# A two-bank Gelu in the perceptron of a window-attention layer on one Trainium2 core

## The chip, the cores and the metric

The kernel runs on one core of one Trainium2 chip. The metric is the device time of one launch in microseconds, as the median of several runs; lower is better. Of the core's engines four do the work here: PE (TensorE, matrix products; its weight loads are listed apart as PEld), ACT (ScalarE, functions from a table), DVE (VectorE) and SP (SyncE, which issues nearly all DMAs).

## The reference, cut to what matters

Four layers follow each other on x of shape (4, 16, 512, 512) in f32. The change is in layer 0 alone; layers 1 to 3 (convolutions with batch norm, a residual block, and a perceptron over channels) are left as they are.

```python
# layer 0
x = x + depthwise_conv3x3(x, pos_w) + pos_b
for each 8x8 window (64 tokens of 16 channels), 2 heads of 8:
    q, k, v = split(affine1(window) @ qkv_w.T + qkv_b)
    out = softmax(q * 8**-0.5 @ k.T) @ v
x = x + out @ proj_w.T + proj_b
h1 = gelu(affine2(x) @ fc1_w.T + fc1_b)     # 16 -> 64 channels
x = x + h1 @ fc2_w.T + fc2_b                # 64 -> 16 channels
```

## The kernel before, in words

`window_attention` does layer 0. The 128 partitions are four groups of 32 (index u, the batch), each of two window rows of 16 channels. A turn n of the main loop takes 64 columns and 8 rows in four places of the image (index vv): for each u and vv, 8 windows of 64 tokens in each of two window rows, so 512 columns of tokens per u and vv. There are 64 turns. The order on PE, DVE, ACT and SP is the order in which the code issues (`manual_schedule`)[...]. Waits are put in by the framework, which knows who wrote and who read each tile.

PSUM has eight banks of 128 x 512 f32. Before, banks 0 to 3 are two tiles of two banks each (`pairs`), and banks 4 to 7 are four tiles of their own (`singles`); `bank(i)` gives bank i of either.

A turn n runs so:

1. `values` (L348, transposes on PE, copied by DVE at L353) and `scores` (L361, into the pairs; Exp on ACT, L369) start the attention of n; between the first and the second `scores` stands `output` of turn n-1 (L428 on PE into banks 5, 7, 4, 6; L433 on DVE adds the residual into `xo`).
2. Seven rounds of `scores`, `attend` (L380, L385 into banks 4 and 5, or 6 and 7), `values` and `divide` (Ln and Exp on ACT at L394 and L395, a product on DVE at L396).
3. `queries` of turn n+1 in two halves (L330; DVE L340 and ACT L338 copy them out to `g`), with the last `attend` and `divide` between.
4. `project` (L404): 32 products into banks 4 to 7, one bank for each u; DVE (L409) adds bank 4+u to `y[:, u]`, four instructions one after the other.
5. The perceptron's first layer for turn n, mixed with the depthwise convolution of turn n+2. 52 slots follow each other. A slot is either one `depthwise` turn (L297: four products of 32x32 by 512 columns, one tap, one u, into bank u of the first two pairs) or one `hidden` turn (L417: four such products with fc1 for one u and vv, into one of banks 4 to 7, then Gelu on ACT at L422 into a `hid` tile). The profile counts each of these f32 products as two records. Slot i works on row group i % 4 of PE. The 16 `hidden` turns stand at slots 4, 6, 9, 11, 14, 16, ..., 36, 39, 41; the other 36 slots are the nine taps of the four u. In the last two turns there is no depthwise work left.
6. The table for Ln and Exp is asked for on ACT (L549), and `position(n + 2)` takes the depthwise result out of the pairs into y: DVE for u = 0 and 2 (L312), ACT for u = 1 and 3 (L308). The next turn's `scores` write into the same pairs.

The table for Gelu is loaded where the first Gelu of a turn needs it; the framework puts the load there (it appears under L422).

Of the kernel before, what the change touches and what calls it, by code (L numbers as in the profile page):

```python
# [12 lines left out]
F32 = mybir.dt.float32  # L13
BF16 = mybir.dt.bfloat16
AF = mybir.ActivationFunctionType
# [10 lines left out]
P = 128  # L26
# [128 lines left out]
def window_attention(ctx: ExitStack, tc, xw, x1, hots, m, v, peak):  # L155
# [14 lines left out]
    nc = tc.nc  # L170
    U = V = 4
    BW = 64
    NJ = BW // WS
    N = NJ * T
# [3 lines left out]
    STEPS = SR // WS * NQ * 2  # L178

    wts = ctx.enter_context(tc.tile_pool(name="w0w", bufs=1))  # L180
    ps = ctx.enter_context(tc.tile_pool(name="w0p", bufs=1, space=PSUM))

    pairs = [ps.tile([P, 2, 512], F32, name=f"pair{i}") for i in range(2)]
    singles = [ps.tile([P, 512], F32, name=f"bank{i}") for i in range(4)]

    def bank(i):
        return pairs[i // 2][:, i % 2, :] if i < 4 else singles[i - 4]

    def quad(i):
        return slice(32 * i, 32 * i + 32)  # L190
# [3 lines left out]
    def load(k):  # L194
        t = xin.tile([P, V, WS + 2, XW + 2], F32, tag="x", name=f"x{k}")
        nc.sync.dma_start(t, xw[k])
        return t
# [6 lines left out]
    def prod(lhsT, rhs, name, n=P):  # L204

        b = bank(7)[:, 0:n]
        nc.tensor.matmul(b, lhsT, rhs, start=True, stop=True)
        t = scratch.tile([P, n], F32, name=name)
        nc.vector.tensor_copy(t, b)
        return t  # L210

    def times(a, s, name):
        t = scratch.tile(list(a.shape), F32, name=name)
        nc.vector.tensor_scalar(t, a, s, None, ALU.mult)
        return t

    def plus(a, b, name, pool=None):
        t = (pool or scratch).tile(list(a.shape), F32, name=name)
        nc.vector.tensor_tensor(t, a, b, ALU.add)
        return t  # L220

    def kept(a, name):
        t = wts.tile(list(a.shape), F32, name=name)
        nc.vector.tensor_copy(t, a)
        return t
# [8 lines left out]
    with tc.tile_pool(name="w0s", bufs=1) as scratch:  # L234
# [11 lines left out]
        for h in range(NH):  # L246
# [11 lines left out]
        fc1 = kept(prod(m("color2"), times(m("fc1"), v("alpha2"), "fc1_a"), "fc1_0"), "fc1_e")  # L258
        f1b = plus(
            prod(m("fc1")[0:32], v("beta2")[0:32], "f1_b", 1), v("fc1_b"), "f1b"  # L260
        )

        pb = plus(pb, v("fc2_b"), "pb2", wts)
        f1b = plus(f1b, prod(fc1[0:32], times(v("fc2_b"), -1.0, "f2n")[0:32], "f2_b", 1), "f1b2", wts)
# [8 lines left out]
    px = ctx.enter_context(tc.tile_pool(name="w0x", bufs=2))  # L273
# [12 lines left out]
    def by_window(ap):  # L286
        return ap.rearrange("p (j a x) -> p a j x", a=WS, x=WS)
# [39 lines left out]
    def queries(y, h):  # L327
        for u in range(U):
            for vv in range(V):
                nc.tensor.matmul(  # L330
                    bank(vv)[quad(u)], wg[h][quad(vv)], y[quad(vv), u, :],
                    start=True, stop=True,
                )
        for vv in range(V):
            out = g[:, vv, :, h, :]
            src = bank(vv).rearrange("p (j t) -> p j t", t=T)
            if vv % 2:
                nc.scalar.activation(out, src, AF.Identity, bias=gb[:, h : h + 1])  # L338
            else:
                nc.vector.tensor_scalar(out, src, gb[:, h : h + 1], None, ALU.add)  # L340


    def values(k, n):

        vv, jl = k // 2, 4 * (k % 2)
        b = bank(4 + 2 * (k % 2))
        for jj in range(4):
            nc.tensor.transpose(  # L348
                b[:, P * jj : P * jj + P],
                y2[:, vv, jl + jj].rearrange("p w t -> p (w t)"), m("ident"),  # L350
            )
        t = px.tile([P, 4, P], F32, tag="yt", name=f"yt{n}_{k}", bufs=3)
        nc.vector.tensor_copy(t.rearrange("p j c -> p (j c)"), b)  # L353
        return t

    def scores(k, n):

        vv, jl = k // 2, 4 * (k % 2)
        for jj in range(4):
            for u in range(U):  # L360
                nc.tensor.matmul(  # L361
                    bank(u)[:, P * jj : P * jj + P],
                    y2[quad(u), vv, jl + jj].rearrange("p w t -> p (w t)"),
                    g[quad(u), vv, jl + jj].rearrange("p h t -> p (h t)"),
                    start=True, stop=True,
                )
        e = px.tile([P, U, 4, P], F32, tag="e", name=f"e{n}_{k}", bufs=3)
        for i in range(2):
            nc.scalar.activation(  # L369
                e[:, 2 * i : 2 * i + 2].rearrange("p u j t -> p u (j t)"),  # L370
                pairs[i], AF.Exp,
            )
        return e
# [36 lines left out]
                y[:, u], bank(4 + u), pb, y[:, u], ALU.add, ALU.add  # L410
            )

    def hidden(y, q, vv, n):

        u, b = q // 4, bank(4 + q % 4)
        for k in range(4):
            nc.tensor.matmul(  # L417
                b[quad(k)], fc1[quad(vv), quad(k)], y[quad(vv), u, :],
                start=True, stop=True,
            )  # L420
        hd = px.tile([P, N], F32, tag="hid", name=f"hid{n}_{u}_{vv}", bufs=16)
        nc.scalar.activation(hd, b, AF.Gelu, bias=f1b)  # L422
        return vv, hd

    def output(y, xo, hids, us, banks, n):

        for k, (vv, hd) in enumerate(hids):
            nc.tensor.matmul(  # L428
                bank(banks[k // 4])[quad(vv)], m("fc2"), hd, start=True, stop=True
            )  # L430
        at = BW * (n % 2)
        for u, i in zip(us, banks):
            nc.vector.tensor_tensor(  # L433
                xo[:, u, :, at : at + BW].rearrange("p a (j x) -> p a j x", x=WS),
                by_window(bank(i)), by_window(y[:, u]), ALU.add,
            )
            if n % 2:
                store(xo, n // 2, u)
# [6 lines left out]
    def store(xo, k, u):  # L445
        i, cb = divmod(k, NQ)
        largest.append(
            lambda: nc.vector.tensor_reduce(
                peak[:, U * k + u : U * k + u + 1], xo[:, u], AX.XY, ALU.max,
                apply_absolute_value=True,  # L450
            )
        )
        for vv in range(V):
            for w in range(2):
                r = SR * (2 * vv + w) + WS * i
                _store_block(
                    nc, x1, xo[32 * vv + C * w : 32 * vv + C * w + C, u], u, r,
                    slice(XW * cb, XW * cb + XW), queues if k == STEPS // 2 - 1 else None,
                )
# [35 lines left out]
    last, xo = None, None  # L495
    nc.scalar.preload_act_table_set("natural_log_exp_and_others")
    for n in range(STEPS):
        yts = {k: values(k, n) for k in range(2)}
        es = {0: scores(0, n)}
        if last:  # L500

            output(*last)
        for k in range(1, 8):
            es[k] = scores(k, n)
            attend(es[k - 1], yts[k - 1], k - 1)
            if k > 1:
                yts[k] = values(k, n)
            divide(k - 1, n)
            if k == 3:
                nc.vector.tensor_reduce(  # L510
                    most[:, n : n + 1], ys[n], AX.XY, ALU.max, apply_absolute_value=True
                )
            elif largest:
                largest.pop(0)()
            if k % 2 and n + 1 < STEPS:
                turn_keys(ys[n + 1], k // 2)
        if n + 1 < STEPS:
            queries(ys[n + 1], 0)
        attend(es[7], yts[7], 7)
        divide(7, n)  # L520
        if n + 1 < STEPS:
            queries(ys[n + 1], 1)
        y = ys.pop(n)
        project(y)

        ahead = n + 2 < STEPS
        if ahead and n % 2 == 0 and n // 2 + 2 < STEPS // 2:
            xts[n // 2 + 2] = load(n // 2 + 2)
        if n % 2 == 0:
            xo = px.tile([P, U, WS, XW], F32, tag="xo", name=f"xo{n}", bufs=1)  # L530
        if n + 1 == STEPS:
            flag = bounded()

        at = [4 + 10 * u + d for u in range(U) for d in (0, 2, 5, 7)]
        hids, taken = [], [0] * U
        for i in range(13 * 4):
            if i in at:
                q = len(hids)  # L540
                hids.append(hidden(y, q, i % 4, n))
                if n + 1 == STEPS and q in (5, 9, 13):
                    u = q // 4 - 1
                    output(y, xo, hids[q - 5 : q - 1], (u,), (u,), n)
            elif ahead:
                depthwise(n + 2, taken[i % 4], i % 4)
                taken[i % 4] += 1
        if n + 1 < STEPS:
            nc.scalar.preload_act_table_set("natural_log_exp_and_others")  # L549
        if ahead:  # L550
            ys[n + 2] = position(n + 2)
        last = (y, xo, hids, range(U), (5, 7, 4, 6), n)
# [822 lines left out]
```

## Time and profile before

| what | value |
|---|---|
| three runs | 6373.32, 6380.44, 6388.24 us; median 6380.44 us |
| span of the profiled execution, first to last instruction | 6371.6 us |
| its own time beyond the span | not shown by the page |
| mean granted TensorE clock | 0.983 |
| 0 to 3400 us (layer 0) | PE busy 3333 us, ACT 2627 us, DVE 1574 us, clock 1.00 |
| 3560 to 6371 us (later layers) | PE busy 2695 us, ACT 1329 us, DVE 1541 us, clock 0.98 |

The profile is of one execution of the program. "Busy" means that at least one instruction of the engine was in flight: products on PE are pipelined and overlap, so a PE busy all the time may still be waiting between products. The time of a turn can be read off a timeline, whose start column counts from the first instruction of the span. One turn of the loop, the one near 1000 us, serves as the example below:

| stretch of that turn, us | what runs on PE | PE busy | DVE busy | ACT busy |
|---|---|---|---|---|
| 1002.30 to 1003.66 | end of project, first depthwise slots | 1.36 | 0.81 | 0.60 |
| 1003.66 to 1014.50 | fc1 and depthwise slots | 10.84 | 1.92 | 10.70 |
| 1014.50 to 1016.87 | depthwise slots | 2.37 | 0.27 | 1.95 |
| 1016.87 to 1019.95 | transposes, first scores | 2.68 | 2.34 | 1.49 |
| 1019.95 to 1024.50 | output, second scores | 4.55 | 2.77 | 1.79 |
| 1024.50 to 1052.00 | the attention's rounds, queries, project | 27.50 | 16.95 | 23.55 |

### The profile page before, as it was taken

To read this page: it belongs to the slowest core of one execution; us is meant where nothing else is said; L and a number is where in the kernel's file an instruction comes from. 1 tells how busy PE (TensorE), PEld (TensorE's weight loads), DVE (VectorE), ACT (ScalarE), POOL (GpSimd) and SP (SyncE) were. 2 spreads that over 40 slices of the span, in tenths; PEclk is the share of its full clock that TensorE was granted. 3 is DMA by queue.
4 is the path that set the end of the run, shared out by engine and by line. 5 is a ranking of instruction groups with operands and counts; after the bars stand their busy time and mean duration, and the time that the engine had idled before them with its cause. 6 is when DMAs were issued, how large, how long until landed. Compare 5 with 4: busy or idle time off the path is not lost. (4 is left out here: it accounts for less than half of the span.)

```text
span 6371.6 us, 316872 instructions
## 1 busy us (share of the span) xinstructions
PE 6125.4 (96%) x146976; PEld 3619.7 (57%) x146976; DVE 3189.7 (50%) x4713; ACT 4035.4 (63%) x5602; POOL 151.0 (2%) x127
## 2 busy tenths in 40 slices
PE   8999999999999999999997569999999999999999
PEld 4666666666666666666663445455555555555554
DVE  3444444444444444444444665555555555555555
ACT  4777777777777777777776544444444444444444
POOL 0000000000000000000002510000000000000000
PEclk9999999999999999999998789999999999999999
DMA  3233323333333333333323732222222222222221
GB/s 81 59 76 61 76 60 75 61 75 61 75 61 75 62 74 62 73 63 73 62 57 108 295 129 76 82 82 87 85 83 84 82 83 83 84 83 83 83 72 51
DMA packets 567526, 515.29 MB, mean 81 GB/s; under 512 B 349009, under 2 KB 478353, under 8 KB 545713
## 3 DMA queue, kind: packets, MB, share of 16 engines
q1 hardware_dynamic: 564688, 493.47, 29.7%
q8 instruction: 1154, 18.91, 1.3%
q0 software_dynamic: 1216, 1.05, 0.1%
q14 instruction: 180, 1.47, 0.1%
q10 hardware_dynamic: 288, 0.39, 0.0%
HBM read 225.87 MB, written 134.48 MB: 57 GB/s over the span
## 5 line engine op out<-in xcount | busy, mean ns | idle before, releaser
L1166 ACT ACTIVATE hid<-tb,vec 128x512 f32<-128x512 f32 x1280 | 830.6, 689 | 1061.0 <-PE tb L1160 1058.1
L1160 PE MATMUL tb<-y,mat 32*32 32x512 f32 x16384 | 1498.8, 596 | 2.0 <-issue 1.5
L369 ACT ACTIVATE e<-pair 128x1024 f32<-128x1024 f32 x1024 | 992.5, 1021 | 396.3 <-PE pair L361 396.3
L1168 DVE TENSOR_SCALAR hid<-tb,vec 128x512 f32<-128x512 f32 x768 | 574.7, 749 | 739.1 <-PE tb L1160 732.9
L297 PE MATMUL pair<-x,taps 32*32 32x512 f32 x18432 | 927.9, 605 | 2.4 <-ACT y L308 1.2
L417 PE MATMUL bank<-y,fc_e 32*32 32x512 f32 x8192 | 680.3, 598 | 1.3 <-DVE y L409 0.9
L361 PE MATMUL pair<-g,y 32*128 32x128 f32 x16384 | 654.0, 285 | 27.1 <-ACT y L308 24.5
L361 PEld LDWEIGHTS pair<-g,y 32*128 32x128 f32 x16384 | 544.1, 187 | 216.1 <-issue 110.8
L297 PEld LDWEIGHTS pair<-x,taps 32*32 32x32 f32 x18432 | 601.8, 103 | 98.5 <-issue 18.8
L422 ACT ACTIVATE hid<-bank,f1b 128x512 f32<-128x512 f32 x1024 | 644.2, 686 | 13.0 <-PE bank L417 5.5
L930 PE MATMUL tb<-z,cw 32*32 32x512 f32 x12864 | 635.2, 600 | 5.4 <-issue 4.1
L353 DVE COPY yt<-bank 128x512 f32<-128x512 f32 x512 | 347.8, 689 | 552.2 <-PE bank L348 533.1
L1160 PEld LDWEIGHTS tb<-y,mat 32*32 32x32 f32 x16384 | 466.5, 103 | 264.1 <-issue 149.8
L930 PE MATMUL tb<-h,cw 32*32 32x512 f32 x12672 | 567.9, 597 | 4.4 <-issue 2.8
L930 PE MATMUL tb<-x,cw 32*32 32x512 f32 x12480 | 562.4, 597 | 1.4 <-ACT z L1099 1.4
L380 PE MATMUL bank<-e,yt 128*32 128x128 f32 x16384 | 557.4, 276 | 3.6 <-issue 2.1
L930 PE MATMUL tb<-q,cq 32*32 32x512 bf16 x12672 | 420.2, 454 | 140.8 <-issue 63.2
L396 DVE TENSOR_TENSOR o<-bank,r 128x512 f32<-128x512 f32 x512 | 354.3, 692 | 372.4 <-ACT r L395 356.2
L385 PE MATMUL bank<-e,hot 128*32 128x512 f32 x4096 | 535.9, 593 | 0.0
L380 PEld LDWEIGHTS bank<-e,yt 128*32 128x32 f32 x16384 | 418.2, 109 | 112.4 <-DVE yt L353 52.8
L1176 PE MATMUL tb<-hid,mat 128*32 128x512 f32 x4096 | 452.7, 594 | 0.0
L312 DVE TENSOR_SCALAR y<-pair,vec 128x512 f32<-128x512 f32 x128 | 90.3, 747 | 707.1 <-PE pair L297 707.1
(163 smaller groups left out, 6689.3 us busy)
## 6 DMA issues: line engine op xcount, KB each, us to landing
x<-in_xw_dram SPq DMA_DIRECT2D x32, 2600.0 KB, 11.0
y<-y SPq DMA_DIRECT2D x2048, 32.0 KB, 2.2
tx<-x SPq DMA_DIRECT2D x64, 1024.0 KB, 5.6
xi<-x SPq DMA_DIRECT2D x1024, 64.0 KB, 2.4
out_dram<-xi SPq DMA_DIRECT2D x64, 1024.0 KB, 4.6
x<-xo SPq DMA_DIRECT2D x1974, 32.0 KB, 1.7
y<-x SPq DMA_DIRECT2D x24, 1024.0 KB, 4.9
xi<-x SPq DMA_DIRECT2D x24, 1024.0 KB, 4.9
```

The costliest lines, as they stand in the source:

```text
L297: nc.tensor.matmul(bank(u)[quad(vv)], taps[quad(u), tap, :], xts[n // 2][quad(u), vv, dy : dy + WS, at : at + BW], start=tap == 0, stop=ta ...
L361: nc.tensor.matmul(bank(u)[:, P * jj : P * jj + P], y2[quad(u), vv, jl + jj].rearrange("p w t -> p (w t)"), g[quad(u), vv, jl + jj].rearra ...
L369: nc.scalar.activation(e[:, 2 * i : 2 * i + 2].rearrange("p u j t -> p u (j t)"), pairs[i], AF.Exp,)
L380: nc.tensor.matmul(b[quad(u), P * jj : P * jj + P], yt[:, jj, quad(u)], e[:, u, jj, :], start=True, stop=True,)
L385: nc.tensor.matmul(d[quad(u)], own, e[:, u].rearrange("p j t -> p (j t)"), start=True, stop=True,)
L417: nc.tensor.matmul(b[quad(k)], fc1[quad(vv), quad(k)], y[quad(vv), u, :], start=True, stop=True,)
L422: nc.scalar.activation(hd, b, AF.Gelu, bias=f1b)
L930: nc.tensor.matmul(p[i][_quad(j)], weights[_quad(i), side, dx, :], src[side][_quad(i), j, dx : dx + W], start=side == 0 and dx == 0, stop= ...
L1160: nc.tensor.matmul(p[_quad(c)], w1[_quad(b), 1 - par, 32 * c : 32 * c + 32], inner(ys(mm + par))[_quad(b), s, :], start=True, stop=True,)
L1166: nc.scalar.activation(hd, p, AF.Relu, bias=v("l3_b1"))
L1168: nc.vector.tensor_scalar(hd, p, v("l3_b1"), 0.0, ALU.add, ALU.max)
L1176: nc.tensor.matmul(p[_quad(b), :], w2[:, par], hd, start=par == 0, stop=par == 1)
```

## The change

All eight banks of layer 0 become four pairs: banks 4 and 5 are one tile, and so are 6 and 7. `hidden` takes two vv at once: eight products into the two banks of a pair, then one Gelu over 128 x 1024 into one `hid` tile of twice the size (half as many buffers, so the same memory). A turn has eight such double turns, at slots 4, 10, 16, ..., 46, each taking the place of two slots; the four slots between two of them stay depthwise. The order of row groups, i % 4, stays as it was. The table for Gelu is asked for explicitly behind the second half of `queries`, ahead of `project`. In the last turn, the calls of `output` follow the new count.

```diff
-    pairs = [ps.tile([P, 2, 512], F32, name=f"pair{i}") for i in range(2)]
-    singles = [ps.tile([P, 512], F32, name=f"bank{i}") for i in range(4)]
+    pairs = [ps.tile([P, 2, 512], F32, name=f"pair{i}") for i in range(4)]
 
     def bank(i):
-        return pairs[i // 2][:, i % 2, :] if i < 4 else singles[i - 4]
+        return pairs[i // 2][:, i % 2, :]
...
-    def hidden(y, q, vv, n):
-
-        u, b = q // 4, bank(4 + q % 4)
-        for k in range(4):
-            nc.tensor.matmul(
-                b[quad(k)], fc1[quad(vv), quad(k)], y[quad(vv), u, :],
-                start=True, stop=True,
-            )
-        hd = px.tile([P, N], F32, tag="hid", name=f"hid{n}_{u}_{vv}", bufs=16)
-        nc.scalar.activation(hd, b, AF.Gelu, bias=f1b)
-        return vv, hd
+    def hidden(y, q, vvs, n):
+
+        u, pair = q // 4, pairs[2 + q // 2 % 2]
+        for j, vv in enumerate(vvs):
+            for k in range(4):
+                nc.tensor.matmul(
+                    pair[quad(k), j], fc1[quad(vv), quad(k)], y[quad(vv), u, :],
+                    start=True, stop=True,
+                )
+        hd = px.tile([P, 2, N], F32, tag="hid", name=f"hid{n}_{q}", bufs=8)
+        nc.scalar.activation(hd, pair, AF.Gelu, bias=f1b)
+        return [(vv, hd[:, j]) for j, vv in enumerate(vvs)]
...
             queries(ys[n + 1], 1)
+        nc.scalar.preload_act_table_set("gelu_and_others")
         y = ys.pop(n)
         project(y)
...
-        at = [4 + 10 * u + d for u in range(U) for d in (0, 2, 5, 7)]
+        at = range(4, 52, 6)
         hids, taken = [], [0] * U
         for i in range(13 * 4):
             if i in at:
                 q = len(hids)
-                hids.append(hidden(y, q, i % 4, n))
-                if n + 1 == STEPS and q in (5, 9, 13):
+                hids += hidden(y, q, (i % 4, i % 4 + 1), n)
+                if n + 1 == STEPS and q in (4, 8, 12):
                     u = q // 4 - 1
-                    output(y, xo, hids[q - 5 : q - 1], (u,), (u,), n)
-            elif ahead:
+                    output(y, xo, hids[q - 4 : q], (u,), (u,), n)
+            elif i - 1 not in at and ahead:
                 depthwise(n + 2, taken[i % 4], i % 4)
                 taken[i % 4] += 1
```

## The prediction

> **What bounds the kernel now.** I read the page first, then the timelines of PE, ACT and DVE over one turn of layer 0's loop (the 64 turns repeat to a few ns; their period is 52.7 or 53.0 us), then who waited for line 308.
>
> ```profile
> span 6371.6 us, 316872 instructions
> PE 6125.4 (96%) x146976; PEld 3619.7 (57%) x146976; DVE 3189.7 (50%) x4713; ACT 4035.4 (63%) x5602; POOL 151.0 (2%) x127
> L422 ACT ACTIVATE hid<-bank,f1b 128x512 f32<-128x512 f32 x1024 | 644.2, 686 | 13.0 <-PE bank L417 5.5
> ```
>
> PE is 96% busy and ACT 63%: shares alone say that a shorter Gelu (L422) saves nothing unless PE waits for it. So the order inside a turn decides. ACT from the end of the queries to the next attention (columns: start, time covered, line and operation, idle before and what ended it):
>
> ```profile
> 1001.55 1.35 ACT L338 ACTIVATE g<-pair,gb 128x512 f32<-128x512 f32 x2 [1.42 <-DVE g L340]
> 1003.68 1.28 ACT L422 ACT_TABLE_LOAD   x1 [0.78 <-DVE y L409]
> 1004.98 10.19 ACT L422 ACTIVATE hid<-bank,f1b 128x512 f32<-128x512 f32 x16
> 1015.18 1.28 ACT L549 ACT_TABLE_LOAD   x1
> 1017.39 1.34 ACT L308 ACTIVATE y<-pair,vec 128x512 f32<-128x512 f32 x2 [0.92 <-DVE y L312]
> ```
>
> ACT looks saturated by Gelus (16 in 10.19 us, one per 0.634), yet it finishes, loads Exp's table and then sits idle 0.92 us before y (L308). PE and DVE over the same stretch:
>
> ```profile
> 1003.66 0.63 PE L417 MATMUL bank<-y,fc_e 32*32 32x512 f32 x4
> 1004.11 0.61 PE L417 MATMUL bank<-y,fc_e 32*32 32x512 f32 x4
> 1013.26 0.66 PE L417 MATMUL bank<-y,fc_e 32*32 32x512 f32 x6
> 1013.78 3.09 PE L297 MATMUL pair<-x,taps 32*32 32x512 f32 x73
> 1018.13 0.49 PE L361 MATMUL pair<-g,y 32*128 32x128 f32 x4 [0.23 <-ACT y L308]
> 1002.85 2.73 DVE L409 SCALAR_TENSOR_TENSOR y<-bank,pb,y 128x512 f32<-128x512 f32 x4 [0.68 <-PE bank L404]
> 1016.60 1.41 DVE L312 TENSOR_SCALAR y<-pair,vec 128x512 f32<-128x512 f32 x2 [11.02 <-PE pair L297]
> ```
>
> The reader is to see the chain: depthwise ends (last record starts 1016.28), DVE y (1016.60 to 1017.35), ACT y (1017.39), scores (L361, 1018.13). The loop numbers 52 slots per turn, each 8 matmul records (four products, each two records); slots 0 to 3 are depthwise, slot 4 is the first fc1 turn. Is PE paced by ACT in there? Two rows say no. The fc1 turn of slot 41 begins at 1013.26 and slot 51 at 1015.83 (1016.28 less 0.457, the gap of a slot's two records): ten slots with nothing to wait for take 0.257 us each; slots 11 to 41 (from DVE's fourth y at 1005.58, plus 0.05, to 1013.26) take 0.254. And where no depthwise remains (the last turn but one) ACT runs 16 Gelus alone:
>
> ```profile
> 3389.93 9.41 ACT L422 ACTIVATE hid<-bank,f1b 128x512 f32<-128x512 f32 x16
> ```
>
> that is one per 0.57 to 0.59, so at 0.634 ACT follows PE. **PE bounds the stretch, at about 0.25 us a slot.**
>
> [...]
>
> **The change part by part**, all in the times of this turn.
>
> 1. *The table load moved.* It is queued right behind the last g (1002.90) and ends near 1004.20 instead of 1004.97. Nothing is removed: two loads a turn remain. Worth nothing: the first Gelu will wait for later things.
>
> 2. *Sixteen Gelus become eight.* [...] (the Exp row of that shape, without a bias, has 1021). ACT's work falls from 16 x 0.686 = 10.98 us to 8.90 by durations; by the cadences from 9.2 free-running to about 8.1. By itself nothing, PE being the pace.
>
> 3. *A pair of banks is one tile to wait for.* In the built order the first fc1 product of a pair carries one wait for DVE and the seven after it none: the pair is waited for as a whole. The project's output (L404) lies in the same pairs. DVE's first y now waits for two banks: the second bank's last record starts 1002.494, ends 1003.08, so y starts 1003.12 instead of 1002.85. fc1 may overwrite the pair when two y are read: 1003.12 + 0.75 + 0.66 = 1004.53, so slot 4 starts at 1004.585 instead of 1003.66. Behind it in PE's queue stand all later depthwise turns: **PE idles 0.93 us**. The second pair's y end at 1005.85, before slot 10 (1006.1): no further stall. Depthwise then ends later by 0.93 less what the early waits cost before: 1004.585 + 47 x 0.25 + 0.457 = 1016.79 against 1016.28, or 0.5.
>
> I take 0.25 us a slot, a little under 0.254 and 0.257, as the array starts empty behind the stall. Lower bound 0.2285: two records of one row group are 0.457 apart (1003.66 and 1004.11 above), four row groups take turns, and both orders rotate them alike. Upper bound 0.265: depthwise alone at the kernel's start (32 records per 1.06 us).
>
> 4. *The last fc1 turn stands at slot 47 instead of 41.* Slot 47 starts 1004.585 + 43 x 0.25 = 1015.34; its second record ends 0.457 + 0.59 later; the last Gelu starts at 1016.44 instead of 1014.48, takes 1.11, ends 1017.55; Exp's table is loaded 1017.57 to 1018.85; ACT y can start at 1018.88, against 1017.39. DVE's y is done by 1017.9, so ACT, which had 0.92 us to spare, now ends the chain: **+1.49 us a turn**. Scores wait for both y of ACT, and all that follows on PE is in order behind them, so the shift stays. Transposes (L348) wait for the last Gelu, 1017.6, and are still done before 1019.6.
>
> 5. *Output (L428) also waits by pairs.* xo's first add waits for two more banks. Before, the adds of DVE start 1021.01, 1021.93, 1022.73, 1023.59; after, from output's start, at 2.85, 3.71, 4.32 and 4.93 us, so the third, the last reader of the first pair, ends at 5.01 instead of 3.54. The first attend, which starts 4.67 after output's start, must wait to 5.07: 0.39 late. The scores behind it stood 0.31 us waiting for ACT's Exp before (1.21 us against 0.90): +0.08 net, bounds 0 and 0.39.
>
> Nothing is added on SP, POOL or a DMA queue; y's transfers are issued many us later and don't notice. A clock drop from PE's gaps (0.9 and about 1.9 us) I cost at nothing: with gaps of up to 0.5 us a turn the granted clock is 1.00; its downside is the upper end.
>
> Sum: (1.49 + 0.08) x 62 turns with depthwise = 97 us, and about 1 for the last two, 98. The page's execution (span 6371.6, what lies around it not shown) would become a span of 6470; the median, 8.8 us above that span, becomes **6478**. Layers 1 to 3 (3400 us onwards) are untouched.
>
> **The rivals.**
> - *Mild*: PE runs near the row groups' limit, 0.2285: slot 47 at 1014.41, ACT y +0.57, sum 0.65 x 62 = 40 us, 6420. Or the stall is smaller, fc1 waiting for the first y alone (1003.93): +0.83 in ACT y, 0.91 x 62 = 56 us, 6437. For: the initial slots do rush at times. Against: 0.254 over 30 slots.
> - *Faster: ACT is the pace*. If fc1's waits for banks hold PE after all, slots shrink until ACT limits: eight Gelus at 1.01 from 1005.7, done 1013.8, load done 1015.1, ACT y 2.3 us earlier, -142 us, 6238. It needs 0.165 us a slot; it decides from (1017.39 - 1.11 - 1.11 - 1.33 - 1004.585) / 43 = 0.215, below which y comes earlier. For: Gelus stand back to back. Against: 0.2285 as the row groups' own limit, and ten free slots at 0.257.
> - *No change*: the waits don't bind as listed and slots take 0.23: ACT y near 1017.4, 6380.
> - *The change doesn't do what it says*: spread and pairing do stand in the built order, and the load does too; it only buys no time, as in 1.
>
> **How the numbers follow.** Likeliest as summed (0.24 to 0.265 a slot) 0.70, mild 0.20, no change 0.04, faster 0.06. 0.2% is 13 us, about what a measurement of this kernel can tell from no change (its three runs span 15). Time 6478. Range: the likeliest reaches up to 2.14 + 0.39 = 2.53 x 62 = 157 us, 6537, of which I keep 6530; below it takes in the mild rival, 6420, with a little room: 6412. Faster 0.06, same 0.05, slower 0.89.
>
> **What would show it.** Gelu x512 at 1.11 us; its load without idle before it; PE's weight loads of fc1 idle 0.9 us a turn for DVE y (0.25 before: 13.5 us in 55 turns); ACT y no longer waiting for DVE y (50.6 us in 55 turns before); PE idle before scores for ACT y up from 0.4 to about 1.9 us a turn; period 54.2. Wrong if slots take under 0.22, if fc1 starts at 1003.7, or if ACT still idles before y.

## The result, and the profile after

| | before | after |
|---|---|---|
| median, us | 6377.12 (6373.32 to 6388.24) | 6498.62 (6492.11 to 6505.04) |
| ratio | | 1.0185, 95% interval 1.017 to 1.0199 |
| span of the profiled execution, us | 6371.6 | 6494.5 |
| end of layer 0 (last add into `xo`) | 3458.4 | 3578.2 |
| rest of the span | 2913.2 | 2916.4 |

The changed kernel is slower by 121 us; 6478 was predicted, in a range of 6412 to 6530. (The ratio 1.0185 is lower than these two medians give, 1.0191; against the median of three runs that stands ahead of the prediction, 6380.44, it comes out.) Nearly all of it lies in layer 0, 119.8 us. Turn by turn that is 0.6 before the first turn, 114.7 in the 62 turns that have depthwise work, and 1.4 and 3.1 in the last two. The median turn went from 52.68 to 54.34 us (+1.66, so 103 us in 62 turns); the other 12 us lie in a few longer turns, which come back below.

The page of the kernel after: the span, the busy times, and the Gelu row.

```profile
span 6494.5 us, 316108 instructions
PE 6159.9 (95%) x146976; PEld 3495.7 (54%) x146976; DVE 3183.0 (49%) x4713; ACT 3948.3 (61%) x5090; POOL 150.6 (2%) x127
L422 ACT ACTIVATE hid<-pair,f1b 128x1024 f32<-128x1024 f32 x512 | 570.1, 1114 | 303.8 <-PE pair L417 303.4
```

Gelu did what the change says: half as many, 1114 ns each, 74 us less ACT work. And ACT now stands idle 303.8 us before them, nearly all of it waiting for PE (13.0 before). That is the answer to "ACT or PE?": the time that Gelu gave up became idle time on ACT. Now ACT's timeline over the turn that starts at 1032.84 (start, time covered, line, operation, idle before it and what ended it):

```profile
1036.49 1.28 ACT L523 ACT_TABLE_LOAD   x1
1039.35 1.11 ACT L422 ACTIVATE hid<-pair,f1b 128x1024 f32<-128x1024 f32 x1 [1.58 <-PE pair L417]
...
1050.19 1.11 ACT L422 ACTIVATE hid<-pair,f1b 128x1024 f32<-128x1024 f32 x1 [0.54 <-PE pair L417]
1051.32 1.28 ACT L550 ACT_TABLE_LOAD   x1
1052.62 1.26 ACT L307 ACTIVATE y<-pair,vec 128x512 f32<-128x512 f32 x2
```

L523 is the moved load of Gelu's table, without any idle ahead of it. From the last Gelu on there is no gap: Gelu, Exp's table (L550), y (L307, line 308 before). The 0.92 us that ACT used to wait for DVE there is gone. DVE's timeline over the same turn has the project's adds and the depthwise y:

```profile
1036.69 2.73 DVE L408 SCALAR_TENSOR_TENSOR y<-pair,pb,y 128x512 f32<-128x512 f32 x4 [0.94 <-PE pair L403]
1050.49 1.58 DVE L311 TENSOR_SCALAR y<-pair,vec 128x512 f32<-128x512 f32 x2 [11.07 <-PE pair L296]
```

and PE's the first fc1 products, the transposes and the scores:

```profile
1038.16 0.66 PE L417 MATMUL pair<-y,fc_e 32*32 32x512 f32 x8 [0.27 <-DVE y L408]
...
1051.14 1.09 PE L347 MATMUL pair<-mat,y 128*128 128x128 f32 x8
1053.36 1.74 PE L360 MATMUL pair<-g,y 32*128 32x128 f32 x32 [1.12 <-ACT y L307]
```

The first fc1 product (L417) waits for DVE's second add and starts 5.32 us into the turn, where it was 4.39. At the other end, DVE's first y (L311) starts at 1050.49, 2.1 us before ACT's: the two no longer meet. PE does the transposes (L347) and then has nothing in flight for 1.12 us, until ACT's y lets the scores (L360) go; it was 0.24 us in the kernel before. Over 400 to 3300 us, 53 turns, the list of waits has (waited for, us in all, times, longest):

```profile
PEld pair L360 <- ACT y L307: 84.9, 104, 1.4
PEld pair L417 <- DVE y L408: 63.3, 53, 1.2
PE pair L360 <- ACT y L307: 58.1, 52, 1.1
```

and the same list for the kernel before, over 55 turns, had for the last two:

```profile
PEld bank L417 <- DVE y L409: 13.5, 55, 0.2
PE pair L361 <- ACT y L308: 21.6, 106, 0.2
```

The same moments of a turn, medians over the 62 turns, counted from the turn's first project product:

| us into the turn | before | after | shift |
|---|---|---|---|
| first fc1 product | 4.394 | 5.315 | +0.921 |
| last depthwise record starts | 17.018 | 17.798 | +0.780 |
| last Gelu ends | 15.90 | 18.48 | +2.58 |
| Exp's table loaded | 17.202 | 19.782 | +2.58 |
| ACT's y starts | 18.124 | 19.794 | +1.670 |
| scores start | 18.864 | 20.535 | +1.671 |
| first Exp starts | 20.539 | 22.129 | +1.590 |
| second `scores` start | 24.183 | 25.773 | +1.590 |
| first `attend` starts | 25.286 | 27.255 | +1.969 |
| fourth `scores` start | 31.021 | 32.683 | +1.662 |
| period | 52.678 | 54.338 | +1.660 |

The chain from the last Gelu moved by 2.58; ACT had 0.92 to spare, and 1.67 was left. Of this 0.08 is won back at once, nearly all of it as ACT's two y start 0.585 us apart and not 0.658; in the kernel before they ran beside DVE's, here they don't. At the first `attend` 0.38 is lost, because the output waits by pairs; most of that is made up for by the fourth `scores`, and 0.07 of it stays in the period.

### The profile page after: what moved, and what is told of

Its sections match the earlier page's. It is cut to its first block, busy times and chain, and to the rows that moved or that the text cites. A ratio compares the mean times of both kernels' runs of the same rounds, so it can differ in the third digit from the quotient of the medians.

```text
span 6494.5 us, 316108 instructions
## 1 busy us (share of the span) xinstructions
PE 6159.9 (95%) x146976; PEld 3495.7 (54%) x146976; DVE 3183.0 (49%) x4713; ACT 3948.3 (61%) x5090; POOL 150.6 (2%) x127
## 3 DMA queue, kind: packets, MB, share of 16 engines
q0 software_dynamic: 1216, 1.05, 0.1%
## 5 line engine op out<-in xcount | busy, mean ns | idle before, releaser
L296 PE MATMUL pair<-x,taps 32*32 32x512 f32 x18432 | 954.3, 604 | 2.1 <-ACT y L307 1.3
L422 ACT ACTIVATE hid<-pair,f1b 128x1024 f32<-128x1024 f32 x512 | 570.1, 1114 | 303.8 <-PE pair L417 303.4
L417 PE MATMUL pair<-y,fc_e 32*32 32x512 f32 x8192 | 717.5, 606 | 20.1 <-DVE y L408 20.1
L360 PE MATMUL pair<-g,y 32*128 32x128 f32 x16384 | 642.1, 286 | 74.4 <-ACT y L307 67.3
L360 PEld LDWEIGHTS pair<-g,y 32*128 32x128 f32 x16384 | 531.3, 188 | 263.6 <-issue 110.0
L352 DVE COPY yt<-pair 128x512 f32<-128x512 f32 x512 | 347.5, 688 | 537.6 <-PE pair L347 523.4
L379 PE MATMUL pair<-e,yt 128*32 128x128 f32 x16384 | 556.9, 276 | 22.7 <-DVE xo L433 19.4
L296 PEld LDWEIGHTS pair<-x,taps 32*32 32x32 f32 x18432 | 474.6, 103 | 187.3 <-issue 67.2
L384 PE MATMUL pair<-e,hot 128*32 128x512 f32 x4096 | 536.0, 593 | 0.0
L395 DVE TENSOR_TENSOR o<-pair,r 128x512 f32<-128x512 f32 x512 | 354.0, 691 | 322.1 <-ACT r L394 305.9
L379 PEld LDWEIGHTS pair<-e,yt 128*32 128x32 f32 x16384 | 418.3, 110 | 135.2 <-DVE yt L352 52.8
L311 DVE TENSOR_SCALAR y<-pair,vec 128x512 f32<-128x512 f32 x128 | 95.6, 750 | 715.3 <-PE pair L296 710.0
```

Of the source, the lines that this page charges most:

```text
L296: nc.tensor.matmul(bank(u)[quad(vv)], taps[quad(u), tap, :], xts[n // 2][quad(u), vv, dy : dy + WS, at : at + BW], start=tap == 0, stop=ta ...
L360: nc.tensor.matmul(bank(u)[:, P * jj : P * jj + P], y2[quad(u), vv, jl + jj].rearrange("p w t -> p (w t)"), g[quad(u), vv, jl + jj].rearra ...
L379: nc.tensor.matmul(b[quad(u), P * jj : P * jj + P], yt[:, jj, quad(u)], e[:, u, jj, :], start=True, stop=True,)
L384: nc.tensor.matmul(d[quad(u)], own, e[:, u].rearrange("p j t -> p (j t)"), start=True, stop=True,)
L417: nc.tensor.matmul(pair[quad(k), j], fc1[quad(vv), quad(k)], y[quad(vv), u, :], start=True, stop=True,)
L422: nc.scalar.activation(hd, pair, AF.Gelu, bias=f1b)
```

## The experiments

The theory: two things cost time, the pair as one unit to wait for (PE's stall at the first fc1) and the place of the last fc1 turn (the chain last Gelu, Exp table, y). The rivals: the load's move or the merged Gelus themselves cost; or output's wait by pairs does; or PE's clock does. In each table below, "turn" is the median of the 62 turns (52.68 before, 54.34 after). The gap is the longest regular one from the transposes to the end of the first `scores`; it lies ahead of the scores but for the three marked with a star, where it lies inside them. "Half-clock windows" counts stretches of 3.41 us between 80 and 3150 us in which the granted clock is 0.5.

| run | median, us | ratio to before, 95% interval | turn, us | PE's gap at the scores, us | half-clock windows |
|---|---|---|---|---|---|
| before | 6377.12 | 1 | 52.68 | 0.24 | 0 |
| after | 6498.62 | 1.0185 (1.017 to 1.0199) | 54.34 | 1.12 | 7 |
| load move alone | 6376.79 | 1.0003 (0.9993 to 1.0013) | 52.68 | 0.24 | 0 |
| spread alone | 6431.10 | 1.0091 (1.0074 to 1.0108) | 53.52 | 0.70 | 2 |
| Exp table later | 6414.39 | 1.0082 (1.006 to 1.0104) | 53.24 | 0.19* | 0 |
| slots 8 to 46 | 6498.83 | 1.0198 (1.0181 to 1.0215) | 54.06 | 1.12 | 17 |
| slots 8 to 46, gap filled | 6464.26 | 1.0145 (1.0125 to 1.0164) | 54.04 | 0.25 | 0 |
| after, short add | 6461.01 | 1.0122 (1.0105 to 1.0139) | 53.51 | 1.26 | 13 |
| before, short add | 6362.86 | 0.9975 (0.9966 to 0.9985) | 52.43 | 0.17 | 0 |
| slots 8 to 42 | 6398.11 | 1.0029 (1.0021 to 1.0038) | 52.78 | 0.11 | 0 |
| slots, table, output | 6389.04 | 1.0018 (1.0011 to 1.0026) | 52.63 | 0.19* | 0 |
| adds over two banks | 6376.68 | 1.0007 (0.9998 to 1.0016) | 52.63 | 0.19* | 0 |

The ratios are against runs of the kernel before on the same chip (medians of 6373 to 6379), so they, not the medians, are to be compared.

**Load move alone.** The kernel before with one line:

```diff
+        nc.scalar.preload_act_table_set("gelu_and_others")
         y = ys.pop(n)
```

> The kernel before, and only the request for Gelu's table added behind the queries. Theory (the load buys nothing, since ACT follows PE in the fc1 stretch and has 0.92 us to spare before y): 6377 us, within 10 us; the first Gelu of a turn starts 0.2 us earlier (at 5.5 us after the turn's first project product instead of 5.71), the last one where it was, 15.2. Rival (ACT paces the stretch): up to 1.28 us x 62 turns gained, 6300 us; and if the earlier load did harm the queries, slower than 6390.

It is no different from before. Its ACT timeline, in the turn that starts near 1000, shows why:

```profile
1003.63 1.28 ACT L523 ACT_TABLE_LOAD   x1
1005.50 1.35 ACT L422 ACTIVATE hid<-bank,f1b 128x512 f32<-128x512 f32 x2 [0.58 <-PE bank L417]
...
1018.10 1.34 ACT L308 ACTIVATE y<-pair,vec 128x512 f32<-128x512 f32 x2 [0.92 <-DVE y L312]
```

The load is done early and ACT then waits 0.58 us for the first products; at the end ACT still waits the same 0.92 us for DVE. The early load buys an idle ACT.

**Spread alone.** The kernel before, single banks and sixteen Gelus, with the fc1 turns at the changed slots:

```diff
-        at = [4 + 10 * u + d for u in range(U) for d in (0, 2, 5, 7)]
+        at = [i + j for i in range(4, 52, 6) for j in range(2)]
```

> The kernel before with its sixteen single fc1 turns and single banks, put at the slots of the changed kernel (4, 5, 10, 11, ..., 46, 47). Theory (two causes: waiting for a pair of banks as one tile stalls PE about 0.9 us; the late last turn brings Gelu and Exp's table onto the chain): the placing alone remains, slot 47 starts 0.75 us earlier than in the changed kernel, the last Gelu is 0.43 us shorter; ACT y starts 0.76 us later than before, 62 x 0.76 = 47 us: 6424 us. If the pairing alone were the cause: 6377. If the placing alone were the cause: about 6490.

Its ACT timeline, in the turn that starts at 1014.01:

```profile
1027.74 3.99 ACT L422 ACTIVATE hid<-bank,f1b 128x512 f32<-128x512 f32 x6 [0.62 <-PE bank L417]
1031.75 1.28 ACT L549 ACT_TABLE_LOAD   x1
1033.05 1.27 ACT L308 ACTIVATE y<-pair,vec 128x512 f32<-128x512 f32 x2
```

The chain without a gap is there with no pairs at all, and y starts 19.04 us into the turn, +0.92. The turn grew by 0.84. But this is not the price of the last fc1 turn's place alone, as had been meant: the new slots also put the second fc1 turn right behind the first, where it waits for DVE's second add. PE's weight loads show it in the same turn:

```profile
1019.06 0.13 PEld L417 LDWEIGHTS bank<-y,fc_e 32*32 32x32 f32 x5 [0.51 <-DVE y L409]
```

From 400 to 3300 us fc1's weight loads wait 40.6 us for DVE's adds, against 13.5 in the kernel before, and the last depthwise record starts 0.46 us later. So 0.84 is the price of the new slots as a whole, with some of the stall in it.

**Exp table later.** The kernel after, with Exp's table asked for behind the y of `position`:

```diff
-        if n + 1 < STEPS:
-            nc.scalar.preload_act_table_set("natural_log_exp_and_others")
         if ahead:
             ys[n + 2] = position(n + 2)
+        if n + 1 < STEPS:
+            nc.scalar.preload_act_table_set("natural_log_exp_and_others")
```

> The changed kernel, but Exp's table is asked for behind position's two ACT instructions instead of ahead of them. Theory (last Gelu, then the load, then ACT y is the chain): ACT y then waits for DVE y again, which ends with depthwise 0.8 us later than before the change; ACT y starts 0.78 us later than before instead of 1.67, and the load hides behind the first scores: 48 us, with some 8 us for the clock windows seen in the changed kernel 6430 us. Rival (the shift comes from PE's late depthwise or from the output's waits, the load is beside the path): no change, 6498.

Its ACT timeline, in the turn that starts at 1007.00:

```profile
1024.35 1.11 ACT L422 ACTIVATE hid<-pair,f1b 128x1024 f32<-128x1024 f32 x1 [0.56 <-PE pair L417]
1025.43 1.52 ACT L307 ACTIVATE y<-pair,vec 128x512 f32<-128x512 f32 x2
1026.97 1.28 ACT L552 ACT_TABLE_LOAD   x1
1028.27 1.94 ACT L368 ACTIVATE e<-pair 128x1024 f32<-128x1024 f32 x2
```

The load (1026.97) now lies between y and the first Exp, and the scores run beside it. The turn gives back 1.09 of 1.66 us: the table really was in the chain. The gain is larger than expected (6430): y starts 18.45 us into the turn, where 18.90 had been expected. It does wait for DVE, as expected, and starts 0.035 us behind the end of DVE's first y in every turn; but that end came only 0.33 us later than before, although the last depthwise record came 0.78 later.

**The stall alone.** The kernel after, with the first double turn at slot 8, behind DVE's adds, and the last one where it was:

```diff
-        at = range(4, 52, 6)
+        at = (8, 14, 20, 26, 32, 34, 40, 46)
```

> The changed kernel with its double turns at slots 8, 14, 20, 26, 32, 34, 40, 46: the first stands where both y are ready, the last where it was. Theory: PE's stall of 0.92 us at the first fc1 turn goes; slot 47 starts at 15.33 us after the turn's first project product instead of 16.26, so ACT y starts 0.76 us later than before instead of 1.67: 47 us, 6424. Rival (the pair wait is hidden, the tail alone decides): 6498. Rival (paired fc1 turns slow PE itself): stays above 6460.

This expectation failed: 6498.83, as slow as the kernel after. The median turn fell by only 0.28 us. ACT's timeline (turn from 1030.94):

```profile
1043.83 2.12 ACT L422 ACTIVATE hid<-pair,f1b 128x1024 f32<-128x1024 f32 x2 [0.29 <-PE pair L417]
1048.02 1.11 ACT L422 ACTIVATE hid<-pair,f1b 128x1024 f32<-128x1024 f32 x1 [0.71 <-PE pair L417]
1049.15 1.28 ACT L550 ACT_TABLE_LOAD   x1
1050.45 1.26 ACT L307 ACTIVATE y<-pair,vec 128x512 f32<-128x512 f32 x2
```

and its list of waits (400 to 3300 us):

```profile
PE pair L360 <- ACT y L307: 54.7, 50, 1.1
PEld pair L417 <- ACT hid L422: 37.4, 53, 0.7
```

The choice of slots brought its own stall. The double turns at 32 and 34 stand back to back, the two Gelus of 1043.83 do too, and the weight loads of fc1 stand idle for a Gelu 0.7 us in every turn. That ate most of what the later first turn had saved, and y still starts only at 19.50. And the granted clock fell more often, 17 windows instead of 7: that kept the total where it was (62 turns of -0.28 make -17 us, ten more windows of 1.6 us make +16).

**Does the gap before the scores drop the clock?** The kernel before had no such window in these turns and the gap was 0.24 us. Here is one of the seven in the kernel after, in the view by stretch (its bounds and length; PE, PEld, DVE, ACT and POOL busy with counts; granted clock, DMA share, GB/s), in a turn that starts at 212.21 and so has its gap at about 231.6 to 232.7:

```profile
229.92:233.33 3.41, 2.20 (x25) 1.16 (x14) 2.64 (x4) 3.32 (x4) 0.00 (x0) 1.00 0.32 44
233.34:236.75 3.41, 3.41 (x36) 2.16 (x40) 0.00 (x0) 1.70 (x2) 0.00 (x0) 0.50 0.35 49
236.75:240.00 3.25, 3.25 (x40) 1.02 (x36) 0.96 (x2) 0.24 (x1) 0.00 (x0) 1.00 0.36 51
```

PE is busy 2.20 of 3.41 us in the stretch that holds the gap, and gets half the clock in the next. A turn with such a window takes 55.93 us instead of 54.33, so 1.6 more. To test it, the previous kernel was run with the transposes for the first two values issued twice, into the same place, which fills the gap and changes no other wait:

```diff
-        for jj in range(4):
+        for jj in [0, 1, 2, 3] * (2 if k < 2 else 1):
```

> As e4_start8_end46, whose PE stands idle 1.12 us ahead of the scores of a turn and whose granted clock fell to half in 17 stretches of 3.41 us in the loop: the eight transposes of the first two values of a turn are issued twice with the same result, 0.8 us more work for PE in that gap. Theory (it is the gap that brings the half clock, 1.6 us lost each time): few or no such stretches left, the period of an undisturbed turn as it was (54.06 us), 17 x 1.6 = 27 us less: 6472. Rival (the half clock follows from something else, or more work simply costs more): 6498 or above, up to 62 x 0.8 = 50 us more.

Of its list of waits (400 to 3300 us), the line that stood at 54.7 us:

```profile
PE pair L360 <- ACT y L307: 12.5, 50, 0.3
```

More work on PE, and 34.6 us less time. The median turn stays (54.06, 54.04), no window of half clock is left, and what turns take above their median falls from 44 to 18 us in all (18 in the kernel before). In the profiled executions layer 0 ends 29.5 us earlier. So here it is the gap that brings the half clock (17 windows with it, none with it filled), though not in every turn that has it. It is a cost of its own, apart from the wait that makes the gap.

**How much is the wait for a pair?** In the kernel after, DVE's four adds of the project work on 64 of 512 columns only, so that the second add of a pair ends early (part of the computation is left out):

```diff
-                y[:, u], bank(4 + u), pb, y[:, u], ALU.add, ALU.add
+                y[:, u, 0:64], bank(4 + u)[:, 0:64], pb, y[:, u, 0:64], ALU.add, ALU.add
```

> The changed kernel, but DVE's four adds of project's result to y treat 64 of 512 columns (the other columns keep the y of before attention, so part of the computation is left out): the wait of fc1 for both y is nearly taken away, slots and Gelus stay as they are. Theory: slot 4 starts 0.85 us earlier, all that follows too; ACT y starts 0.8 us later than before the change instead of 1.67: 50 us, 6425. Rival (the stall is made up for later in the stretch, and the tail alone counts): 6490 or more.

and as a control the same edit in the kernel before:

> The control: the kernel before with the same short adds (64 of 512 columns, part of the computation left out). Theory: fc1's first four turns waited for DVE y there too, but cost at most 0.2 us a turn: 6363, between 6360 and 6377. If short adds gain 0.8 us a turn here as well (6325), g3_short_add says nothing about pairs.

The kernel after loses 0.83 us a turn by it, the kernel before 0.25. With the stall gone, fc1's weight loads wait for DVE 14.3 us in all (63.3 in the kernel after), the first fc1 product starts at 4.385, as before the change, and ACT (turn from 1019.14) has the same chain, earlier:

```profile
1035.68 1.12 ACT L422 ACTIVATE hid<-pair,f1b 128x1024 f32<-128x1024 f32 x1 [0.61 <-PE pair L417]
1036.82 1.28 ACT L550 ACT_TABLE_LOAD   x1
1038.11 1.27 ACT L307 ACTIVATE y<-pair,vec 128x512 f32<-128x512 f32 x2
```

The turn takes 53.51 us, and so does the kernel with the spread alone (53.52). One has pairs and eight Gelus without the stall, the other single banks and sixteen Gelus; the table starts 17.68 and 17.74 us into the turn. This tie is partly chance: the last Gelu is 0.43 us longer with pairs, while the single banks wait longer for DVE. The cleaner comparison is between the two kernels with the short add. In both the last depthwise record starts 16.84 us into the turn, so the adds hold up neither more than the other; yet the turns are 53.51 and 52.43. These 1.08 us are the price of the late last turn with its longer Gelu, the 0.07 of the output among them. The other 0.58 of the 1.66 (0.83 less the control's 0.25) is the wait for a pair. The median of 6461 is above the expected 6425 though the turn is what was expected; 13 windows of half clock, at a gap of 1.26 us, are in it.

**Both causes taken away.** Three kernels go back toward before while keeping the pairs and the eight Gelus. The first puts the double turns at slots 8 to 42, two u in turn, so that each comes at least four slots behind the one before and 42 is the last:

```diff
-        at = range(4, 52, 6)
+        at = {8: 0, 12: 1, 18: 0, 22: 1, 28: 2, 32: 3, 38: 2, 42: 3}
...
-                hids += hidden(y, q, (i % 4, i % 4 + 1), n)
+                hids[at[i]] += hidden(y, at[i], done, (i % 4, i % 4 + 1), n)
```

> The changed kernel with its double turns at slots 8, 12, 18, 22, 28, 32, 38, 42 (u in the order 0, 1, 0, 1, 2, 3, 2, 3), so that no two stand back to back. Theory (stall at the first double turn, and the late last one): both go; PE waits only a little for Gelus (0.2 us a turn); slot 42 starts near 14.4 us after the turn's first project product, ACT y starts 0.2 us later than before: 6390 us, within 15. Rival (paired turns slow PE in themselves, or the pairs' waits do so throughout): 6450 or more.

The turn is 52.78 us: of the 1.66, 1.56 are gone. The last turn is 9.1 us longer from its start to its last add (29.9, 20.8 before), as its outputs stand behind the loop. The second also asks for Exp's table behind y and takes the banks of `output` in the order of the pairs:

```diff
-        last = (y, xo, hids, range(U), (5, 7, 4, 6), n)
+        last = (y, xo, hids, range(U), (5, 4, 7, 6), n)
```

> As g1_slots_8_to_42, and also Exp's table asked for behind position's two ACT instructions, and output's banks in the order 5, 4, 7, 6, so that DVE's first two adds need one pair alone. Theory: ACT y waits for DVE y as before the change, 0.15 us later than there; PE no longer waits for xo before the first attend: 6380, within 10, about as before. Rival: as g1 or slower, if the late table now delays the first Exp.

Now 62 turns take 1.6 us less in all than before; the last turn takes 6.5 more, and the later layers 7 more in the profiled execution. The third has DVE add two banks at once (two instructions instead of four, as the pair is waited for whole anyway) and moves most of the last turn's outputs back into the loop:

```diff
-        for u in range(U):
+        for i in range(2):
...
-                y[:, u], bank(4 + u), pb, y[:, u], ALU.add, ALU.add
+                y[:, 2 * i : 2 * i + 2], pairs[2 + i], pb, y[:, 2 * i : 2 * i + 2],
+                ALU.add, ALU.add,
```

> As g2_slots_table_output, with DVE's four adds of project's result made two over a pair of banks each, and the last turn's outputs put back inside the loop. Theory: the pair's y is read in about 1.28 us instead of 1.41, so fc1 starts 0.1 to 0.15 us a turn earlier (6 to 9 us), and the last turn's end regains about 6: 6374, within 8 of the kernel before on either side. Rival (PE is at its pace from slot 0 on and the first double turn didn't wait): 6383.

In its last turn the two adds over 128 x 1024 took 2.48 us together, so about 1.24 for a pair, where 1.28 was expected. The kernel is a tie with the one before: 1.0007, interval 0.9998 to 1.0016. The time was met, but not in the way expected: fc1 does start earlier (5.19 us into the turn, 5.32 in the second), yet the turn stays at 52.63, and the last turn is still 7 us longer than before. Of the 8.6 us between the profiled executions of the second and the third, 7 lie in the later layers, which neither touches; the intervals of the two ratios overlap. No kernel that computes the whole beats the one before. The best that pairs and merged Gelus came to here, with the waits that they made mostly taken away again, is no gain: half as many Gelus were worth nothing here, where PE sets the pace.

## Why the prediction was right

The direction and the two mechanisms were right, and the size nearly: 121 us measured, 98 predicted. By the prediction's own steps:

1. *The load moved*: worth nothing, predicted and measured alone (1.0003).
2. *Half the Gelus*: 1.11 us each predicted, 1114 ns found; nothing gained. The kernel before allows the same estimate: its Ln over 128 x 512 (L394) takes 596 ns and its Exp over 128 x 1024 (L369) 1021, and the difference of 425 on top of Gelu's 686 makes 1111; eight of these are 8.89 us, and 8.90 was forecast for ACT. ACT's idle time before them shows it on the page; by experiment, the turns of 52.63 us do, which have eight Gelus and gain next to nothing on 52.68.
3. *A pair as one wait*: fc1 at 5.32 us into the turn predicted, 5.315 found; gone with the short add. The 0.93 us is the shift of fc1, though, and not idle time of PE: PE's products overlap (those of one fc1 slot, from 1003.66 in the kernel before, start 0.45 us apart and last 0.59 each), so in the stall nothing is in flight for 0.27 us only. And the depthwise turns behind fc1 did wait with it (the next starts at 5.38 us).
4. *The last fc1 turn at slot 47*: here is the first mis-sized term. The prediction took 0.25 us a slot behind the stall; slots 4 to 47 took 0.255, so slot 47 came 0.22 us later than forecast; 0.18 of it reached y, at +1.67 instead of +1.49. In 62 turns that is 11 us. "The array starts empty behind the stall", a guess of the prediction, bought nothing; the rate before, 0.254, was nearly the right one to take. Bounds of 0.2285 and 0.265 held it. What the step left out is that ACT's two y then follow each other 0.08 us faster, 5 us less in 62 turns.
5. *Output's wait by pairs*: right. PE waits there now, as the page's row shows (before, then after), 19.4 us in 64 turns or 0.30 each:

```profile
L380 PE MATMUL bank<-e,yt 128*32 128x128 f32 x16384 | 557.4, 276 | 3.6 <-issue 2.1
L379 PE MATMUL pair<-e,yt 128*32 128x128 f32 x16384 | 556.9, 276 | 22.7 <-DVE xo L433 19.4
```

The first `attend` starts 0.38 us late by the table of moments, where 0.39 was predicted, and 0.07 stays, where 0.08 was. With the single banks of "spread alone" the shift is 0.84 from the first Exp to the period, with nothing lost here; with `output`'s banks in the order of the pairs (second kernel of the last group) the loss is gone.
6. *A clock drop, costed at nothing*: the second mis-sized term. Seven windows of 1.6 us are 11 us. The gap itself was forecast, as 1.9 us; 1.12 was found, as the transposes run in part of that stretch.
7. The last two turns cost 4.5 us, not 1. The later layers took 3 us more; the change doesn't touch them, and over these runs they vary by up to 22 us.

So 98 + 11 (slots) - 5 (closer y) + 11 (clock) + 3.5 + 3 = 121.5. Of the rivals, "mild" wanted slots at the 0.2285 us that it estimated for the row groups or a wait for one add only, and "ACT is the pace" wanted under 0.215 us a slot; 0.255 decides against both.

One kernel with a gap of 1.12 us had 7 windows of half clock, another 17. The traces show what sets their turns apart. All drops of a trace stand on one grid of 3.413 us (to within 0.01 us, before and after). Take the line of this grid that follows the end of the gap. In these two kernels 22 turns have it 0.45 to 1.0 us behind the gap, and all 22 lose a window; of the other turns two do, at 0.41 and, in the very first turn, at 1.72 us. With the short add, all 12 turns that have it at 0.40 to 1.05 us lose one, and one other turn, at 1.85. With the spread alone and its gap of 0.70 us only two do, at 0.79 and 0.83. So in these runs the gap cost time almost only where it fell rightly on a grid that the turns, of another length, drift along; how often that happened differs from kernel to kernel. Nine of the 16 spaces between drops in the kernel of 17 are 163.84 us, 48 times 3.413, which is three turns of 54.06 and one of the losses of 1.6 us.

Two things stay open: why the line came so far behind the gap where a window was lost, and what holds PE at 0.255 us a slot when the prediction's estimate, half of the 0.457 us between two records of one row group, is 0.2285. Neither was tried.

## What to carry to other kernels

Before making an engine's instructions fewer and larger, ask which wait ends last, and whether that engine sets the pace: here 74 us less Gelu on ACT gained nothing, and ACT's idle time before Gelu went from 13.0 to 303.8 us. Joining buffers into one tile joins their waits: price the first user against the last writer of the whole tile, with everything that stands in order behind that user (0.58 us a turn here). Where a stretch ends in a table switch, look at what precedes the switch: here an even spread of the same sixteen Gelus alone made the turn 0.84 us longer, with some of the stall at the first fc1 in it.

## What was not expected of the hardware

A gap of about 1.1 us in PE's work was enough, where it fell rightly on the grid of 3.413 us, to get half the clock for 3.41 us afterwards. PE was not idle for all of the window before it: in the kernel after, it was busy for 2.20 of 3.41 us in the one from 229.92, and the next had a clock of 0.50. In some 58 turns, regular gaps of at most 0.31 us a turn gave no window, 0.70 gave 2, and 1.12 to 1.26 gave 7 to 17; each cost about 1.6 us, and filling the gap with useless transposes removed them all.
